# A delta-rule attention block on one core: x is fetched and added ahead of a batch's closing sums, and the gates of the next batch are spread over the second half of their step

## The chip, the cores and the metric

The kernel runs on one core of one Trainium2 chip. The metric is device time in microseconds (us) for one execution. Before the change the runs gave a median of 3071.77 us (three runs, 3068.05 to 3073.72).

## The reference, cut to what matters

The input x has 4 batches of 512 tokens of 512 features. The block is a chain of four parts, each of which reads the one before:

```
c   = bi_wkv(r=x, k=fside, v=fside, w, u, cond)        # scan over time, both ways
a   = gated_delta_rule(c)                              # W_qkvz, W_ba, conv of 4 taps, 16 q/k heads, 32 v heads
      g    = -exp(A_log) * softplus(a_proj + dt_bias)  # the gates, one per token and v head
      beta = sigmoid(b_proj)
      g summed within a chunk; T = (I + tril(beta k k' * exp(g_i - g_j)))^-1 ...
x1  = x + rmsnorm(o) * norm_w * silu(z) @ W_out'       # summed over all heads
h   = bi_wkv(r=x1, ...)                                # the second one, same form
out = x1 + h @ (sign(W) * mean|W|)' + bias             # a binarized weight
```

## The kernel before

**Units and steps.** The work of the attention is cut into units n = b*16 + hq: one batch and one q/k head, with its two v heads; there are 64. A unit is handled in chunks of 128 tokens, four to a batch. The kernel runs through steps i = 1 to 66, and step i works on several units at once: letters in the plan say how far off they are. F is unit i (projections, taps of the convolution, inverse), C is unit i-1 (the recurrence over four chunks), O is unit i-2 (norm and head turns), W is unit i-3 (the product with W_out), and K is unit i+6 (key norms and the matrix that is to be inverted). The units of a group of four are inverted together, in 30 small sub-steps on GpSimd, 1 to 20 in one step and 21 to 30 in the next; that comes every fourth step.

**The order is written by hand.** `plan` (L1173 to L1242) is a list of 22 slots, and in each slot a list of calls. All engines get their instructions in the order of these calls, through the helper `InOrder` (L75 to L80), so that each row of the profile says L80, and an operation is told by the names of its tiles. `job(i, slot, f, ...)` appends a further call behind those of a slot in step i. Items of the plan that begin with "wkv" or "gate" run only in the steps in which a slice of bi-WKV or the gates of the next batch are due; the gates come with head 8, which is in steps 8, 24 and 40, and prepare batches 1, 2 and 3.

**The gates.** `gates_product` (L305) puts the two projections of W_ba into PSUM (ps_ba). `gates_exp` (L321) makes beta's exponential, y and e = exp(-|y|). `gates_series` (L341) works out log(1+e) as a series on VectorE in three parts: 0 is s = e/(e+2) and its square, 1 is nine operations on p, and 2 is four operations that end in y, the gate. `gates_beta` (L336) finishes beta. `gates_sum` (L362) takes three matmuls that sum y within a chunk (ps_g). `gates_keep` (L369) makes eg = exp of those sums on ScalarE, a copy of the sums (gsum) on ScalarE, the negative copy (gsum) and a reordered copy (sp_f) on VectorE. `gates_turn` (L386) transposes sp_f on TensorE (ps_gt), and `gates_rows` (L391) copies it to rows and stores these in DRAM (gsc), from where each later unit loads its row, spread over all partitions, as dkd (`gap_load`, L593, through SyncE's queue). `gap_mask` (L601) masks dkd on GpSimd and `gap_exp` (L609) takes its exponentials on ScalarE, four instructions in each of two halves.

**The product with W_out and its closing sums.** It is done by a scheme of seven products of half size; `out_add` (L1034) adds the seven results of each unit into seven accumulators: parts 2 to 5 lie in xs[b], parts 1, 6 and 7 in sums[b]. When the last unit of a batch is through, `out_close` (L1055) turns these into the sum over heads: seven additions in the order of `CLOSE`, then four that add x, one for each row block of 128 tokens. `out_load` (L1051) fetches x for that into the tile x_again. xs[b] is then stored as x1[b] (for batches 0 to 2) through SyncE's queue, and the second bi-WKV and the last product work from it. The jobs at L1658 to L1663 place them: in step 18, 34 and 50 for batches 0, 1 and 2, and in step 65 for the last one, where the tail of the kernel follows (`last_turn`, `last_mix`, `last_product`, `last_add`).

**Buffers.** x_again uses the tag "raw" of pool `ld`, four buffers shared by the slices of bi-WKV (`load_slice`, L211) and a few weights. PSUM has banks "pj" (three), "pp" (two), "inv" (one) and "st" (two).

Other names that the prediction uses: `inverse_1` to `inverse_4` (L742 to L807) finish the inverse of unit F on TensorE with copies on VectorE (inv_t, nw); `key_norm` (L621) and `key_root` (L628) make 1/|k| from sums of squares, the start on VectorE (kn, rs_t_k, rs_y_k) and the iterations on GpSimd; `out_norm` and `out_root` (L972, L977) do so for the output (rs_y_o), and `out_scale` (L980) uses it; `taps` and `tap` (L515 to L529) are the convolution on VectorE (y); `z_product` (L857) the gate of the output (ps_z); `chunk_r`, `chunk_w` and `chunk_t` (L882 to L941) the recurrence, with tiles r, state, nw, qs and o.

Of the kernel before, what the change touches and what calls it, by code (L numbers as in the profile page):

```python
# [12 lines left out]
ALU = mybir.AluOpType  # L13
# [27 lines left out]
def kernel(  # L41
# [21 lines left out]
    B, S, D = x.shape  # L63
# [4 lines left out]
    NC = S // P  # L68
# [14 lines left out]
    V, A, G, T, Q = (InOrder(e) for e in (nc.vector, nc.scalar, nc.gpsimd, nc.tensor, nc.sync))  # L83
# [36 lines left out]
    for i in range(3):  # L120
        t = const.tile([P, NM, P], F32, name=f"inv_t{i}")
        G.memset(t, 0.0)
        inv_t.append(t)
        t = const.tile([P, NM // 2, 3 * BS], F32, name=f"inv_n{i}")
# [21 lines left out]
    with ExitStack() as main:  # L146
# [13 lines left out]
        xs, cT, beta, gsum, eg = {}, {}, {}, {}, {}  # L160
# [863 lines left out]
        def out_sum(b, i):  # L1024


            if i in (1, 6, 7):
                return sums[b][:, (1, 6, 7).index(i)]
            t, dh = {2: (0, 0), 3: (0, 1), 4: (1, 0), 5: (1, 1)}[i]
            return xs[b][:, 2 * t : 2 * t + 2, dh * D2 : (dh + 1) * D2]  # L1030

        sums = {}
# [13 lines left out]
            if i == 6:  # L1046
                del units[n]

        CLOSE = ((6, 1), (2, 1), (3, 5), (3, 6), (7, 6), (4, 7), (5, 7))

        def out_load(b, c):  # L1051
            raw = sums["x", c] = ld.tile([P, D], F32, tag="raw", name=f"x_again_{b}_{c}")
# [1 line left out]

        def out_close(b, i):  # L1055

            if i < len(CLOSE):
                to, more = (out_sum(b, j) for j in CLOSE[i])
                V.tensor_tensor(to, to, more, ALU.add)
                return  # L1060
            for c in (2 * (i - len(CLOSE)), 2 * (i - len(CLOSE)) + 1):
                V.tensor_tensor(xs[b][:, c], xs[b][:, c], sums["x", c], ALU.add)
            if i > len(CLOSE) and b < B - 1:
                Q.dma_start(out=x1[b], in_=xs[b])


# [97 lines left out]
        def last_add(b, c):  # L1164
# [7 lines left out]
        K, F, C, O, W = AHEAD, 0, -1, -2, -3  # L1172
# [14 lines left out]

            [(chunk_r, C, 1), (inverse_2, F), (out_add, W, 3), 
             (chunk_r_end, C, 1), (slab_end, K, 1), (chunk_q_end, C, 1),
             (gap_exp, F, "t", 1), ("gate", gates_series, 0), ("sub", 3, 23)],  # L1190

            [(out_product, W, 5), (project, K, 1, 0), (slab_turn, F, 2), ("wkv", turn_slice, "x"),
             (inverse_2_end, F), (out_add, W, 4), (out_scale, O, 1), ("wkv", wkv_bound), ("gate", gates_series, 1),
             ("sub", 4, 24)],

            [(chunk_w, C, 1), (project, K, 1, 1), (head_turn, O, 0), (out_product, W, 6), (chunk_w_end, C, 1), (out_add, W, 5), 
             (slab_end, F, 2), ("wkv", wkv_exp), ("wkv", wkv_x),
             (slab_start, F, 3), ("gate", gates_series, 2), ("gate", gates_beta), ("sub", 5, 25)],

            [(project, F, 2, 0), (out_add, W, 6), (tap, K, 1, 0), (taps, K, 1), (head_end, O, 0),  # L1200
             ("wkv", wkv_mix), ("sub", 6, 26)],

            [(chunk_t, C, 1), (inverse_3, F), ("gate", gates_sum), (chunk_t_end, C, 1), (silu, K, 1),
             ("wkv", wkv_scan, "d", False), (slab_start, F, 0), ("sub", 7, 27)],

            [(project, F, 2, 1), (head_turn, O, 1), (slab_turn, F, 3), ("gate", gates_keep), (inverse_3_end, F), ("wkv", wkv_scan, "d", True),
             (square, K, 1), (chunk_squares, C, 1), ("sub", 8, 28)],

            [(chunk_r, C, 2), (inverse_4, F), (norms, K, 1), (tap, F, 2, 0), (head_end, O, 1), (slab_end, F, 3), (tap, F, 2, 1),
             (chunk_r_end, C, 2), (tap, F, 2, 2), (tap, F, 2, 3), (norms_copy, K, 1), (chunk_q_end, C, 2),  # L1210
             ("wkv", wkv_sum, "d"), (slab_start, C, 4), (slab_start, C, 5), ("gate", gates_turn), ("sub", 9, 29)],

            [(project, F, 3, 0), (norms_turn, K, 1), (slab_turn, F, 0), (inverse_4_end, F), (silu, F, 2), ("gate", gates_rows),
             ("wkv", wkv_scan, "n", False), ("sub", 10, 30)],

            [(chunk_w, C, 2), (project, F, 3, 1), (chunk_w_end, C, 2), (key_norm, K), (key_root, K),
             (slab_end, F, 0), ("wkv", wkv_scan, "n", True), ("sub", 11, None)],

            [(project, F, 0, 0), (turn, F, 2), (tap, F, 3, 0), (taps, F, 3), ("store",), ("wkv", wkv_sum, "n"), (out_start, O, 0), ("sub", 12, None)],

            [(chunk_t, C, 2), (slab_turn, C, 4), (chunk_t_end, C, 2), (silu, F, 3),
             (turn_end, F, 2), ("soon", load_slice), ("wkv", wkv_under), ("sub", 13, None)],

            [(project, F, 0, 1), (turn, F, 1), (slab_turn, C, 5), (slab_end, C, 4),
             (chunk_squares, C, 2), (head_forms, O), (out_start, O, 1), ("sub", 14, None)],

            [(chunk_r, C, 3), (key_pairs, K), (tap, F, 0, 0), (slab_end, C, 5), (turn_end, F, 1),
             (tap, F, 0, 1), (chunk_r_end, C, 3), (tap, F, 0, 2), (tap, F, 0, 3),
             (chunk_q_end, C, 3), (inverse_load, F + 1), ("sub", 15, None)],

            [(z_product, C, 0, 0), (turn, F, 3), (key_matrix, K, 0), (silu, F, 0), ("sub", 16, None)],

            [(chunk_w, C, 3), (z_product, C, 0, 1), (out_turn, O, 0), (chunk_w_end, C, 3),
             (turn_end, F, 3), (square, F, 0), (key_matrix, K, 1), ("wkv", wkv_over, 0),
             (gap_load, K + 1, "d"), (slab_start, K + 1, 1), ("sub", 17, None)],

            [(z_product, C, 1, 0), (out_turn, O, 1), (out_end, O, 0), (key_blocks, K), ("wkv", wkv_over, 1), ("sub", 18, None)],

            [(chunk_t, C, 3), (norms, F, 0), (queries, F), (z_silu, C, 0), (out_end, O, 1),
             (out_forms, O), ("wkv", wkv_end), ("sub", 19, None)],  # L1240
# [15 lines left out]
        for pool, tag, count, shape in (  # L1256
# [3 lines left out]
            for i in range(count):  # L1260
                t = pool.tile(shape, F32, tag=tag, name=f"lent_{tag}_{i}")
# [6 lines left out]
        for pool, tag, shape in ((u1p, "nz", [P, NC, 2, HD]), (u1p, "hT", [P, 7, S // 2])):  # L1268
            t = pool.tile(shape, F32, tag=tag, name=f"lent_{tag}")
# [361 lines left out]
        def job(i, slot, f, *args):  # L1631
            jobs.setdefault((i, slot), []).append((f, args))
# [3 lines left out]
        for n in range(KT):  # L1636
            i, slot = at + n // 2, 9 * (n % 2)
# [3 lines left out]
        for b in range(B - 1):  # L1641
            i = at + 2 + 2 * b
# [15 lines left out]
        for b in range(B):  # L1658
            i = b * HQ + HQ + 2 if b < B - 1 else NU + 1
            for c in range(NC):  # L1660
                job(i, 6 + 3 * c, out_load, b, c)
            for n in range(len(CLOSE) + 2):
                job(i, 5 + n + max(0, n - len(CLOSE) + 1) * 3, out_close, b, n)  # L1663

        def last_step():
            n = NU - 1
# [40 lines left out]
        for i in range(1, NU - W - 1):  # L1707
            b, hq = divmod(i, HQ)
# [62 lines left out]
```

## Time and profile before

| | |
|---|---|
| runs before, median (lowest to highest) | 3071.77 us (3068.05 to 3073.72) |
| profiled execution, its own time | 3063.65 us |
| its span | 3061.9 us |
| mean granted TensorE clock | 0.982 |
| an ordinary step late in the run (step 56) | 42.34 us |
| steps with gates: 8, 24, 40 | 56.47, 53.43, 53.57 us |
| steps with a batch's sums: 18, 50 | 42.34, 42.34 us |
| the steps after these: 19, 35, 51 | 53.17, 53.17, 45.51 us |
| from the start of step 64 to the end | 79.9 us |

The profile is of one execution; it lies 8.1 us under the median of the runs. PE is the matmul engine (TensorE), PEld its weight loads, DVE is VectorE, ACT is ScalarE, POOL is GpSimd, SP is SyncE with its DMA queue. The first steps, with batch 0, last some 45.6 to 46 us each, as the products with the weights are accompanied by their preparation there. In a row of the timeline, "[3.14 <-ACT gsum L80]" means that the engine was idle for 3.14 us before that instruction, until ACT's instruction on gsum let it go. PEclk is the granted clock as a share of full speed.

### The profile page before, as it was taken

The page shows a single profiled execution, that of the slowest core. Times are in us where ns is not written, and L with a number is a line of the kernel's source. Part 1 is how long each engine was busy: PE and PEld are TensorE (multiplying, and loading weights), DVE is VectorE, ACT ScalarE, POOL GpSimd, SP SyncE. Part 2 cuts the span into 40 slices and gives each one's busy share as a digit, 9 for nine tenths or more (in the row PEclk, how much of TensorE's full clock was granted, in tenths as well). Part 3 has the DMA queues.
Part 4 walks back from the last instruction along what each step waited for, and adds up shares of the span by engine and source line. Part 5 has one row for each costly group of instructions (what it writes and reads, how often), then busy time and mean ns, then how long its engine had stood idle before and what let it go on. Part 6 is the DMA issues. An engine that isn't in the chain of part 4 may idle for free.

```text
span 3061.9 us, 60269 instructions
## 1 busy us (share of the span) xinstructions
PE 2949.3 (96%) x20816; PEld 2126.5 (69%) x20816; DVE 2279.0 (74%) x5101; ACT 1879.8 (61%) x5145; POOL 1479.1 (48%) x3249
## 2 busy tenths in 40 slices
PE   8689999999999999999999999999999999999998
PEld 4457776777777677677777677777777677766765
DVE  7858777778767788788867788788876767688754
ACT  3657666666666666666666566666666566656552
POOL 3126464564634556265543646356553525265313
PEclk9789999999999999999999999999999999999999
DMA  5325444454453433334333433434433332333422
GB/s 139 91 84 163 128 147 129 139 168 122 139 162 119 129 95 114 91 92 131 95 110 111 131 86 98 114 99 119 117 94 118 102 110 92 113 112 107 124 87 75
DMA packets 422464, 351.75 MB, mean 115 GB/s; under 512 B 219856, under 2 KB 337616, under 8 KB 421776
## 3 DMA queue, kind: packets, MB, share of 16 engines
q1 hardware_dynamic: 420240, 347.27, 38.6%
q8 instruction: 167, 2.74, 0.4%
q14 instruction: 137, 1.12, 0.1%
q10 hardware_dynamic: 1920, 0.62, 0.1%
HBM read 268.87 MB, written 78.91 MB: 114 GB/s over the span
## 4 chain that ended last, share of the span: by engine, by line
PE 77%; DVE 10%; ACT 5%; POOL 5%; issue 2%; DMA 2%; SPq 0%; POOLq 0%; ACTq 0%; DVEq 0%
PE ps_p L80 24%; PE ps_z L80 12%; PE ps_out L80 11%; PE ps_s L80 4%; PE ps_w L80 4%; PE ps_o L80 3%; DVE y L80 3%; PE ps_st L80 2%; PE ps_j L80 2%; PE ps_kq L80 2%; PE ps_f L80 2%; PE ps_kk L80 2%; PE ps_v L80 2%; PE ps_i L80 1%; POOL L L80 1%
## 5 line engine op out<-in xcount | busy, mean ns | idle before, releaser
L80 PE MATMUL ps_p<-cT,w 128*128 128x512 f32 x2000 | 955.1, 606 | 14.0 <-ACT w L80 11.7
L80 DVE SCALAR_TENSOR_TENSOR y<-ps_p,cw,y 128x511 f32<-128x511 f32 (+2 forms) x768 | 572.0, 745 | 268.7 <-ACT y L80 254.0
L80 PEld LDWEIGHTS ps_p<-cT,w 128*128 128x128 f32 x2000 | 358.1, 193 | 316.3 <-issue 271.3
L80 PE MATMUL ps_out<-wo,hS 128*128 128x256 f32 (+1 forms) x1780 | 462.2, 393 | 24.8 <-ACT k L80 14.0
L80 PE MATMUL ps_z<-w,cT 128*128 128x256 f32 x2048 | 478.0, 380 | 5.1 <-ACT w L80 5.1
L80 PEld LDWEIGHTS ps_z<-w,cT 128*128 128x128 f32 x2048 | 375.0, 191 | 48.3 <-ACT w L80 5.4
L80 PEld LDWEIGHTS ps_out<-wo,hS 128*128 128x128 f32 x1780 | 314.0, 192 | 74.1 <-ACT k L80 14.8
L80 ACT ACT_TABLE_LOAD x153 | 196.3, 1283 | 189.5 <-DVE y L80 167.7
L80 POOL TENSOR_TENSOR rs_t_k<-rs_y_k 128x4 f32<-128x4 f32 x171 | 56.8, 332 | 497.5 <-DVE rs_y_k L80 489.0
L80 POOL TENSOR_TENSOR L<-L,t 128x30 f32<-128x30 f32 (+14 forms) x450 | 250.8, 557 | 34.8
L80 DVE TENSOR_TENSOR x<-x,ps_out 128x512 f32<-128x512 f32 x240 | 163.2, 683 | 138.9 <-PE ps_out L80 138.8
L80 POOL TENSOR_TENSOR t<-L 128x30 f32<-128x30 f32 (+14 forms) x450 | 229.2, 509 | 30.9 <-DMA L<-blocks_m 0.4
L80 DVE SCALAR_TENSOR_TENSOR o<-o,rs_y_o,nz 128x128 f32<-128x128 f32 x512 | 196.8, 445 | 16.8 <-POOL rs_y_o L80 16.4
L80 ACT ACTIVATE qs<-ps_s,eg 128x128 f32<-128x128 f32 x384 | 119.9, 363 | 140.0 <-DVE r L80 114.3
L80 ACT ACTIVATE junk<-o 128x128 f32<-128x128 f32 x512 | 157.9, 308 | 75.2 <-DVE o L80 66.9
L80 ACT ACTIVATE y<-ps_p,cw 128x512 f32<-128x512 f32 x256 | 173.9, 680 | 48.0 <-PE ps_p L80 47.8
L80 ACT ACTIVATE dkt<-dkt,gsum 128x128 f32<-128x128 f32 x512 | 162.6, 392 | 58.1 <-POOL dkt L80 57.9
L80 ACT ACTIVATE v<-y 128x512 f32<-128x512 f32 x128 | 80.7, 630 | 189.5 <-DVE y L80 189.4
L80 ACT ACTIVATE wd<-ps_w,eg 128x128 f32<-128x128 f32 x384 | 118.5, 361 | 82.6 <-PE ps_w L80 82.2
L80 ACT ACTIVATE dkd<-dkd,gsum 128x128 f32<-128x128 f32 x512 | 156.4, 388 | 16.9 <-POOL dkd L80 16.2
L80 PEld LDWEIGHTS ps_o<-w,dkt 128*128 128x128 f32 x1024 | 154.2, 192 | 14.7 <-ACT w L80 2.1
L80 ACT COPY w<-ps_w 128x256 f32<-128x256 f32 (+1 forms) x346 | 144.7, 429 | 25.7 <-PE ps_w L80 25.6
(295 smaller groups left out, 5746.0 us busy)
## 6 DMA issues: line engine op xcount, KB each, us to landing
w<-wsc SPq DMA_DIRECT2D x288, 256.0 KB, 5.2
wo<-wosc SPq DMA_DIRECT2D x47, 896.0 KB, 5.0
dkd<-gsc SPq DMA_DIRECT2D x64, 512.0 KB, 4.1
dkt<-gsc SPq DMA_DIRECT2D x64, 512.0 KB, 5.0
wraw<-in_L_attn_W_qkvz_dram SPq DMA_DIRECT2D x96, 256.0 KB, 3.0
wsc<-w SPq DMA_DIRECT2D x90, 256.0 KB, 2.1
wosc<-wo SPq DMA_DIRECT2D x16, 896.0 KB, 3.9
blocks_m<-dkd SPq DMA_DIRECT2D x256, 32.0 KB, 1.9
```

The source lines that it names most:

```text
L80: return lambda *args, **kw: tc.keep_in_program_order(op(*args, **kw))
```

## The change

It moves calls between the slots; no operation is added or removed.

- The gates: series part 0 goes from slot 4 to slot 5, part 1 from slot 5 to slot 11, part 2 from slot 6 to slot 13; the sums from slot 8 to slot 14, right behind `chunk_t` of chunk 2; beta from slot 6 to 15; `gates_keep` from 9 to 16; `gates_turn` from 10 to 17, behind the first half of `z_product`; and the rows with their store from 11 to 19.
- The closing sums: x is fetched in slots 0 to 3, not 6, 9, 12 and 15. The sum (3, 5) comes first, then the four additions of x, then the other six sums: one call per slot, slots 7 to 17. Before, the seven sums stood in slots 5 to 11 and two pairs of additions of x in slots 15 and 19. The store of x1 moves with the last of them, from slot 19 to slot 17, which on SyncE's queue is ahead of dkd's load (slot 18), not behind it.

```diff
-             (gap_exp, F, "t", 1), ("gate", gates_series, 0), ("sub", 3, 23)],
+             (gap_exp, F, "t", 1), ("sub", 3, 23)],
...
-             (inverse_2_end, F), (out_add, W, 4), (out_scale, O, 1), ("wkv", wkv_bound), ("gate", gates_series, 1),
-             ("sub", 4, 24)],
+             (inverse_2_end, F), (out_add, W, 4), (out_scale, O, 1), ("wkv", wkv_bound), ("gate", gates_series, 0), ("sub", 4, 24)],
...
-             (slab_start, F, 3), ("gate", gates_series, 2), ("gate", gates_beta), ("sub", 5, 25)],
+             (slab_start, F, 3), ("sub", 5, 25)],
...
-            [(chunk_t, C, 1), (inverse_3, F), ("gate", gates_sum), (chunk_t_end, C, 1), (silu, K, 1),
+            [(chunk_t, C, 1), (inverse_3, F), (chunk_t_end, C, 1), (silu, K, 1),
...
-            [(project, F, 2, 1), (head_turn, O, 1), (slab_turn, F, 3), ("gate", gates_keep), (inverse_3_end, F), ("wkv", wkv_scan, "d", True),
+            [(project, F, 2, 1), (head_turn, O, 1), (slab_turn, F, 3), (inverse_3_end, F), ("wkv", wkv_scan, "d", True),
...
-             ("wkv", wkv_sum, "d"), (slab_start, C, 4), (slab_start, C, 5), ("gate", gates_turn), ("sub", 9, 29)],
-
-            [(project, F, 3, 0), (norms_turn, K, 1), (slab_turn, F, 0), (inverse_4_end, F), (silu, F, 2), ("gate", gates_rows),
-             ("wkv", wkv_scan, "n", False), ("sub", 10, 30)],
+             ("wkv", wkv_sum, "d"), (slab_start, C, 4), (slab_start, C, 5), ("sub", 9, 29)],
+
+            [(project, F, 3, 0), (norms_turn, K, 1), (slab_turn, F, 0), (inverse_4_end, F), (silu, F, 2),
+             ("wkv", wkv_scan, "n", False), ("gate", gates_series, 1), ("sub", 10, 30)],
...
+            [..., ("wkv", wkv_sum, "n"), (out_start, O, 0), ("gate", gates_series, 2), ("sub", 12, None)],
+            [(chunk_t, C, 2), ("gate", gates_sum), (slab_turn, C, 4), (chunk_t_end, C, 2), (silu, F, 3),
...
+             (chunk_squares, C, 2), (head_forms, O), (out_start, O, 1), ("gate", gates_beta), ("sub", 14, None)],
+             (chunk_q_end, C, 3), (inverse_load, F + 1), ("gate", gates_keep), ("sub", 15, None)],
+            [(z_product, C, 0, 0), ("gate", gates_turn), (turn, F, 3), (key_matrix, K, 0), (silu, F, 0), ("sub", 16, None)],
+            [..., (key_blocks, K), ("wkv", wkv_over, 1), ("gate", gates_rows), ("sub", 18, None)],
...
-        CLOSE = ((6, 1), (2, 1), (3, 5), (3, 6), (7, 6), (4, 7), (5, 7))
+        CLOSE = ((3, 5), (6, 1), (2, 1), (3, 6), (7, 6), (4, 7), (5, 7))
...
-            if i < len(CLOSE):
-                to, more = (out_sum(b, j) for j in CLOSE[i])
-                V.tensor_tensor(to, to, more, ALU.add)
+            if 1 <= i <= NC:
+                V.tensor_tensor(xs[b][:, i - 1], xs[b][:, i - 1], sums["x", i - 1], ALU.add)
                 return
-            for c in (2 * (i - len(CLOSE)), 2 * (i - len(CLOSE)) + 1):
-                V.tensor_tensor(xs[b][:, c], xs[b][:, c], sums["x", c], ALU.add)
-            if i > len(CLOSE) and b < B - 1:
+            to, more = (out_sum(b, j) for j in CLOSE[max(0, i - NC)])
+            V.tensor_tensor(to, to, more, ALU.add)
+            if i == NC + len(CLOSE) - 1 and b < B - 1:
                 Q.dma_start(out=x1[b], in_=xs[b])
...
             for c in range(NC):
-                job(i, 6 + 3 * c, out_load, b, c)
-            for n in range(len(CLOSE) + 2):
-                job(i, 5 + n + max(0, n - len(CLOSE) + 1) * 3, out_close, b, n)
+                job(i, c, out_load, b, c)
+            for n in range(NC + len(CLOSE)):
+                job(i, 7 + n, out_close, b, n)
```

## The prediction

> **What bounds the kernel now.** I read the page first, then stretches of the trace step by step. A step here runs from its first ps_w<-vb matmul to the next step's.
>
> ```profile
> span 3061.9 us, 60269 instructions
> ...
> PE 2949.3 (96%) x20816; PEld 2126.5 (69%) x20816; DVE 2279.0 (74%) x5101; ACT 1879.8 (61%) x5145; POOL 1479.1 (48%) x3249
> ```
>
> TensorE (PE) is busy 96% of the span, so only the steps in which PE idles can change. The busy times of step 56 (nothing special), 24 (gates), 19 and 51 (after a batch's sums), then three fixed clock windows (columns: stretch, length, PE, PEld, DVE, ACT, POOL, PEclk):
>
> ```profile
> 2622.08:2664.42 42.34, 42.34 (x310) 30.80 (x308) 27.46 (x71) 26.20 (x75) 10.61 (x35) 1.00 0.38 106
> 1221.17:1274.60 53.43, 48.60 (x348) 35.83 (x347) 35.53 (x96) 30.57 (x86) 10.96 (x35) 0.97 0.31 86
> 994.68:1047.85 53.17, 46.16 (x317) 33.35 (x316) 38.65 (x79) 29.37 (x77) 35.13 (x70) 0.90 0.38 117
> 2407.17:2452.68 45.51, 42.90 (x310) 30.79 (x309) 30.32 (x69) 27.70 (x76) 24.76 (x64) 1.00 0.42 122
> 1248.00:1251.41 3.41, 0.26 (x4) 0.14 (x5) 0.82 (x3) 3.35 (x9) 0.00 (x0) 1.00 0.00 0
> 1251.41:1254.83 3.42, 3.42 (x27) 1.90 (x27) 2.59 (x6) 2.12 (x7) 0.00 (x0) 0.50 0.02 5
> 2418.77:2422.19 3.42, 1.59 (x7) 1.11 (x8) 3.33 (x10) 2.23 (x10) 2.95 (x7) 1.00 0.00 0
> ```
>
> Step 56 is all PE: 42.34 us is the floor. The granted clock goes by windows of 3.41 us: PE busy 0.26 us in one, and the next is at half speed; busy 1.59, and it is not. A window with 1.30 (2760.11) was followed by 0.50 too. So a gap costs about 1.7 us more when it leaves a window under some 1.4 us of PE. Third, what PE waits for (total us, times, longest), and DVE in step 24:
>
> ```profile
> PE ps_out L80 <- ACT k L80: 14.0, 2, 7.0
> ...
> PE ps_j L80 <- issue: 6.3, 2, 3.2
> ...
> PE ps_w L80 <- DVE r L80: 3.7, 4, 2.6
> PE ps_lx L80 <- DVE x L80: 3.5, 1, 3.5
> ```
> ```profile
> 1250.38 0.29 DVE L80 TENSOR_SCALAR gsum<-ps_g 128x128 f32<-128x128 f32 x1 [3.14 <-ACT gsum L80]
> ```
>
> The 3.2s are steps 24 and 40: DVE holds at gates_keep's gsum until ACT has loaded a table and made eg and gsum; nw behind it is what PE wants. The 7.0s are steps 19 and 35, the 2.6 step 51, the 3.5 the tail.
>
> **Gates (steps 8, 24, 40).** Counts are unchanged; places change. Step 24 = 42.34 + ps_ba 3.64 + ps_g 0.74 + ps_gt 0.27 + idle 0.33, 1.34 and 3.15 (PE's rows) + 1.62 left for the half clock = 53.43.
>
> After: I lay the moved instructions over step 56, shifted by ps_ba's 3.64. DVE ends inverse_4's copies at +28.3 (2646.80 in step 56). Then, in program order, nine p operations 2.9 (starts 58.3 to 61.2 in the first gates), the key-norm trio 0.6, the taps of slab 3 2.3, and series part 2, 1.1: sp_y is ready at +35.1. PE reaches ps_g, now right behind chunk_t 2, at +32.4 (2650.82 in step 56). Idle 2.7. Later ps_gt stands behind the first half of z_0, reached at +41.4; it needs ACT's qs, a table load 1.28, eg 0.49, gsum 0.26, DVE's gsum and sp_f 0.57, ready at +43.0. Idle 1.6. The old 4.82 goes, 4.3 comes: 51.3 without a clock loss, -2.1 each in steps 24 and 40; step 8 (56.47, idle 4.04, same loss) -1.8. Sum -6.1. A 2.7 us gap leaves 0.7 us of a window if it lies inside one, 2.07 if split evenly: I take two drops of three, +3.4. Bounds: none, or three (+5.1). Net **-2.7** (-6.1 to -1.0; if ps_g and ps_gt found half my waits, -12.6). Cost nothing: ACT's table loads, four in the step in the order of instructions before and after; POOL's mask of steps 24 and 40, which that order puts ahead of key_root, since POOL is busy 11 us of 53 there; the rows' store, which goes out later on SP, behind the blocks' stores, but is first read by the dkd load of the next step, 40 us on (without that gap, its landing would hold the mask).
>
> **Batch sums.** Steps 18, 34, 50 have room on PE (42.34). The sums' price falls due one step on. The chain of waits of step 19, and POOL beside and without DVE's adds:
>
> ```profile
> 996.86 5.88 DMA w<-wsc
> 1002.73 0.07 issue
> 1002.80 1.10 POOL dkd L80
> ...
> 1006.37 0.48 ACT k L80
> 1006.84 0.04 issue
> 1006.89 3.78 PE ps_out L80 x8
> ```
> ```profile
> 989.53 1.28 DVE L80 TENSOR_TENSOR x<-x,x_again 128x512 f32<-128x512 f32 x2
> 989.70 1.63 POOL L80 TENSOR_TENSOR L<-L,t 128x238 f32<-128x238 f32 x1
> ```
> ```profile
> 994.98 0.66 POOL L80 TENSOR_TENSOR L<-L,t 128x238 f32<-128x238 f32 x1
> ```
>
> ACT's copy k, which PE waits for, is queued behind eight dkd exponentials; these wait for POOL's mask, queued behind the group's sub-steps and out_root. The dkd load is not it: issued 990.23, landed 994.23, mask 1002.80. POOL is late because sub-steps beside DVE adds of two SBUF tensors stretch: the four x adds (2.57 us) cost it 1.92, 0.75 us per us.
>
> After: x is loaded in slots 0 to 3, and all eleven adds come in slots 7 to 17. DVE is the same up to key_norm; then six adds instead of four stand beside POOL: 2 x 0.68 x 0.75 = +1.05. The mask also falls one root operation later, +0.28. PE idles 8.3 instead of 7.0: +1.3 in each of steps 19 and 35, with the clock's loss about equal (2.8 now, 2.6 then, +-0.85): **+2.6**. Between 0 (stretching ends in sub-steps that are waiting anyway) and +3.4 each. The x1 store, now ahead of the dkd load on SP's queue, holds it until the last add; 8.6 us of slack at the mask cover that; without them each us would be a us. r_3 in steps 18 and 34 waits for DVE at most 0.5: nothing taken.
>
> The Trainium skill ("SBUF — State Buffer", section "Who interferes with whom") says that DVE with two SBUF inputs and GpSimd share a port under an exclusive lock, and that the loser fully blocks. That speaks against the move; by one for one the 1.05 would be 1.36, the forecast 0.6 higher. The measured 0.75 lies under it.
>
> Step 51: PE waits 2.6 for r, behind DVE's out_scale, behind POOL's out_root. The same shift of some 0.8 makes it 3.4, and its window, 1.59 us busy now, falls to about 0.8: clock, +1.7. **+2.5** (0 to +2.7).
>
> **Tail.** x is issued at 3029.45 to 3031.4 and its adds end by 3037.21, PE idle 3.5, then a half clock (2.7 lost).
>
> ```profile
> 3034.25 0.69 DVE L80 TENSOR_TENSOR x<-x,x_again 128x512 f32<-128x512 f32 x1 [1.78 <-DMA x_again<-in_x_dram]
> ...
> 3037.21 1.87 DVE L80 TENSOR_TENSOR x<-x,ps_out 128x512 f32<-128x512 f32 x3
> ```
>
> After: x lies there, and DVE runs eleven adds at 0.68 without that wait, so the first x<-x,ps_out starts at about 3035.85: -1.35. The gap left, 2.2, is at the clock's edge: half of 2.7 saved. **-2.65** (-1.35 to -4.05).
>
> **Sum:** -2.7 + 2.6 + 2.5 - 2.65 = -0.25 on the profiled 3063.65, so 3063.4. The runs' median, 3071.77, lies 8.1 above that execution; the forecast on that scale is **3071.5**.
>
> **Rivals.** *Slower: POOL under DVE's adds.* The six adds cost POOL one for one (1.4, +0.28), and PE's longer gap empties a window more (+1.7): steps 19 and 35 +6.8, r_3 +0.5, step 51 +2.5, all three gate gaps drop the clock (-1.0), the tail gains 1.35 only: +7.4, **3079**. It decides once the gap in step 19 exceeds about 8.5. For it: gaps of 7.0 already halved three windows. Against: the 0.75, and sub-steps with slack.
>
> *Faster: the gates fit.* What decides is DVE's backlog at +28; its row in step 56, 1.31 idle before slab 3's taps, can absorb part of the p operations. Waits halve to 2.15 a step, no drops: -12.6; step 51 unchanged and clock kept in the tail: +2.6 - 4.05. -14, **3058**. If nothing of what is said to be spread waits at all: 6 more off, 3051.
>
> *Clock by gap length.* Only gaps over a whole window drop it: the gates keep 3.4, step 51 1.7, the tail's 2.2 gap keeps 1.35 more. -6.7, **3065**. Against it: the window with 1.30 us of PE, and step 24's gap of 3.15, which dropped it. The Trainium skill ("TensorE: Matmul & The Clock Gate", "HAM oscillation — how this bites in real kernels") gives this rule: "no PE-idle gaps >~3.4µs." By it the time is this rival's; the 3.15 gap does not agree.
>
> *The change does not do what it says:* x's adds simply trade places with sums, DVE's total is the same; that is in the forecast already (closes +5.1, no gain).
>
> **How the numbers follow.** Forecast 0.50, 3066 to 3077; slower 0.24; gates fit 0.14; gap length 0.12. A measurement tells about 0.2%, 6.1 us, from no change. Faster: 0.14, half of 0.12, and 0.03 of the forecast's edge: 0.23. Slower: 0.24 and 0.02 of the forecast's edge: 0.26. Same: 0.51. For 8 in 10 the range leaves out the gates-fit case and the upper end of POOL's: 3063 to 3080.
>
> **What would show it.** Step 24 near 51.3 to 53, with PE waits at ps_g (2.7, DVE sp_y) and ps_gt (1.6, DVE sp_f) and none at ps_j; steps 19 and 35 near 54.5 with 8.3 at ps_out; step 51 near 48; PE reaching ps_lx some 1.3 earlier. A step 19 of 43, or gate steps of 47, would make me wrong towards faster: then the mask, or the p operations, weren't what I think PE waits for. Steps 18, 34 or 50 over 44 would make me wrong towards slower.

## The result and the profile after

The changed kernel takes 3053.48 us (median of 4 runs, 3052.29 to 3055.59), the kernel before 3072.74 in the runs beside it (4 runs): ratio 0.994, 95% interval 0.9923 to 0.9958. It is faster by about 0.6%, the interval leaves out no change, and the time lies 9.5 us under the low end of the range. The first four runs of the kernel before were on the high side: in later sets of 21 and 22 runs its median was 3066.35 and 3066.63, and in a further set the changed kernel came to 3052.60 beside 3067.49 (ratio 0.9959, 0.9946 to 0.9973). So the gain is some 14 to 15 us, or 19 by the first runs. The two profiled executions, 3063.65 and 3053.92, differ by 9.7 us.

Second profiles of both kernels were taken (3068.99 and 3052.60). Lengths of the steps by which they differ, in us:

| steps | before (two profiles) | changed (two profiles) | forecast of the change | measured, mean |
|---|---|---|---|---|
| 19 and 35 | 106.4, 106.8 | 96.9, 96.8 | +2.6 | -9.7 |
| 18, 34 and 50 | 127.0, 127.0 | 129.2, 129.2 | 0 | +2.2 |
| 51 | 45.5, 44.9 | 44.4, 44.4 | +2.5 | -0.8 |
| 8, 24 and 40 | 163.5, 165.7 | 161.0, 161.1 | -2.7 | -3.5 |
| 9 | 46.8, 46.7 | 47.6, 47.7 | 0 | +0.9 |
| 64 to the end | 79.9, 79.4 | 77.8, 76.2 | -2.65 | -2.7 |

The rest is the start and single half-clock windows in steps 1 to 7 and 58 to 62, which come and go between executions of one kernel. In total the gates and the tail came out much as forecast. The closing part is where the forecast failed.

The page of the changed kernel, and then steps 24, 19 and 51 of it, with the columns as in the prediction:

```profile
span 3052.2 us, 60274 instructions
...
PE 2945.0 (96%) x20816; PEld 2124.5 (70%) x20816; DVE 2285.3 (75%) x5101; ACT 1881.6 (62%) x5145; POOL 1475.2 (48%) x3249
```
```profile
1214.16:1267.69 53.53, 48.89 (x349) 35.74 (x348) 36.48 (x96) 30.93 (x86) 11.38 (x35) 0.97 0.31 88
992.41:1040.84 48.43, 44.97 (x317) 32.16 (x316) 39.69 (x79) 29.28 (x77) 34.61 (x69) 0.96 0.43 130
...
2397.19:2441.61 44.42, 43.06 (x309) 30.84 (x308) 31.28 (x71) 27.47 (x76) 24.36 (x63) 1.00 0.47 141
```

The count of instructions on each engine is the same; step 24 is as long as before, and step 19 has lost 4.7 us, with a granted clock of 0.96 in place of 0.90. What PE waits for in the changed kernel, from the list of waits (total us, times, longest):

```profile
PE ps_out L80 <- DVE sums L80: 10.3, 4, 3.5
...
PE ps_g L80 <- DVE sp_y L80: 8.0, 3, 3.3
...
PE ps_gt L80 <- DVE sp_f L80: 4.1, 3, 1.4
...
PE ps_lx L80 <- DVE x L80: 2.1, 1, 2.1
```

The two waits of 7.0 us for ACT's k are gone from the list; in their place PE waits 3.5 for DVE's copy of sums. In step 19 of the changed kernel, first PE, then ACT:

```profile
997.45 1.89 PE L80 MATMUL ps_out<-wo,hS 128*128 128x256 f32 x8
...
1004.35 1.26 PE L80 MATMUL ps_out<-wo,hS 128*128 128x256 f32 x4 [3.46 <-DVE sums L80]
```
```profile
1001.26 2.44 ACT L80 ACTIVATE dkd<-dkd,gsum 128x128 f32<-128x128 f32 x8 [4.77 <-POOL dkd L80]
1003.61 0.56 ACT L80 COPY k<-ps_k 128x512 f32<-128x512 f32 x1
```

ACT still waits for POOL's mask and still copies k last, at 1003.61. But PE does not wait for that: the fourth and fifth product (ps_out x8) run at 997.45, right behind ps_k. Before, the same eight matmuls stood until 1006.89:

```profile
1006.89 3.78 PE L80 MATMUL ps_out<-wo,hS 128*128 128x256 f32 x8 [7.00 <-ACT k L80]
```

The mask starts 50.8 us after the start of step 18 (50.5 before), so the gain is not an earlier mask.

What differs is in the compiled program. The tiles ps_out, ps_k, ps_x and others share three banks of PSUM, and which bank a tile gets is settled when the program is laid out. In steps 19 and 35, in order:

| | product 0 | 1 | 2 | ps_k | product 3 | 4 | 5 |
|---|---|---|---|---|---|---|---|
| before, bank | 0 | 2 | 0 | 1 | **1** | 2 | 0 |
| changed, bank, step 19 | 1 | 0 | 1 | 2 | **0** | 1 | 0 |

Before, product 3 was put into the bank of ps_k, and so could not start until ACT, ps_k's reader, had copied it, behind eight exponentials that waited for POOL's mask. In the compiled program of the kernel before, the first matmul of product 3 does wait for ACT's copy k; after the change it waits for an earlier instruction of DVE. Of all 28 steps of the kernel before that have a ps_k, only 19 and 35 have it so. After the change the late mask is off PE's path, and the next thing late is POOL's out_root, which DVE's out_scale waits for, with the copy of sums behind it.

### The profile page after: what moved, and what is told of

Its sections match the earlier page's. It is cut to its first block, busy times and chain, and to the rows that moved or that the text cites. A ratio compares the mean times of both kernels' runs of the same rounds, so it can differ in the third digit from the quotient of the medians.

```text
span 3052.2 us, 60274 instructions
## 1 busy us (share of the span) xinstructions
PE 2945.0 (96%) x20816; PEld 2124.5 (70%) x20816; DVE 2285.3 (75%) x5101; ACT 1881.6 (62%) x5145; POOL 1475.2 (48%) x3249
## 4 chain that ended last, share of the span: by engine, by line
PE 75%; DVE 10%; POOL 5%; ACT 5%; DMA 2%; issue 2%; SPq 0%; POOLq 0%; ACTq 0%; DVEq 0%
PE ps_p L80 23%; PE ps_z L80 12%; PE ps_out L80 11%; PE ps_w L80 4%; PE ps_s L80 4%; DVE y L80 3%; PE ps_o L80 3%; PE ps_st L80 2%; PE ps_j L80 2%; PE ps_kq L80 2%; PE ps_f L80 2%; POOL t L80 2%; POOL L L80 2%; PE ps_v L80 1%; PE ps_i L80 1%
## 5 line engine op out<-in xcount | busy, mean ns | idle before, releaser
L80 PE MATMUL ps_p<-cT,w 128*128 128x512 f32 x2000 | 958.2, 608 | 16.0 <-ACT w L80 13.6
L80 POOL TENSOR_TENSOR rs_t_o<-rs_y_o 128x8 f32<-128x8 f32 x192 | 38.6, 201 | 256.9 <-DVE rs_y_o L80 232.8
```

Source lines behind the costliest of these rows:

```text
L80: return lambda *args, **kw: tc.keep_in_program_order(op(*args, **kw))
```

## The experiments

Theory A was: the bank is what counts, and the earlier store of x1 is what moves it. Rival B: it is the additions' order, by POOL. Rival C: the gates bring more than their steps show.

**The two parts alone.** Close: only the functions `out_close` and `CLOSE` and the jobs are from the changed kernel. Gates: only the plan.

```diff
-                job(i, 6 + 3 * c, out_load, b, c)
+                job(i, c, out_load, b, c)
...
+                job(i, 7 + n, out_close, b, n)
```
```diff
-            [(chunk_t, C, 1), (inverse_3, F), ("gate", gates_sum), (chunk_t_end, C, 1), (silu, K, 1),
+            [(chunk_t, C, 1), (inverse_3, F), (chunk_t_end, C, 1), (silu, K, 1),
...
+            [(chunk_t, C, 2), ("gate", gates_sum), (slab_turn, C, 4), (chunk_t_end, C, 2), (silu, F, 3),
```

> The kernel before with the closing sums alone moved (new order, x fetched in slots 0 to 3, all eleven additions in slots 7 to 17, store of x1 in slot 17); the gates stay. Theory A: the gain of the closing part comes from which PSUM bank the fourth product of steps 19 and 35 gets: before, that of ps_k, whose reader on ACT is queued behind the masked exponentials; with the store of x1 earlier, another. It expects steps 19 and 35 near 48.4 (53.2 before), steps 18, 34 and 50 some 0.7 longer, step 51 about 1 shorter, the tail 2 shorter: about 10 to 16 us faster than before. Rival B: the additions' new order keeps POOL from being late; the same times, but the mask some 2 us earlier against the start of step 18. Rival C: the gates carry the gain: under 5 us here.

> The kernel before with the gates alone spread; closing sums, x and store as before. Theory A: steps 24 and 40 stay near 53.5 (idle at ps_g about 3.3 and at ps_gt about 1.4 in place of 0.33, 1.34 and 3.15), step 8 falls by 2 to 3; steps 19 and 35 stay near 53.2 as ps_k and the fourth product share a bank there: 1 to 5 us faster in all. Rival C: 9 us or more faster, being the part of the gain that the one profile of before does not show.

Close alone: 3058.06 us against 3066.63, ratio 0.9975 (0.9963 to 0.9986); steps 19 and 35 are 48.3 and 48.2, steps 18, 34 and 50 together 129.2, step 51 44.5. 8.6 us faster, a little under the 10 expected. Gates alone: 3062.38, ratio 0.9988 (0.9979 to 0.9997), 4.3 us faster; step 8 falls from 56.5 to 53.7, steps 24 and 40 stay at 53.7, and steps 19 and 35 stay at 52.8 and 52.6 with the wait for k (7.2). The parts add up: 8.6 + 4.3 = 12.9 of 14. Rival C falls.

**The second pair of additions, and with it the store of x1, earlier in the kernel before.**

```diff
-                job(i, 5 + n + max(0, n - len(CLOSE) + 1) * 3, out_close, b, n)
+                job(i, 5 + n + max(0, n - len(CLOSE) + 1) * 3 - 2 * (n == len(CLOSE) + 1), out_close, b, n)
```

> The kernel before with one thing moved: the second pair of additions of x and with it the store of x1 from slot 19 to slot 17; the seven sums, the gates and the fetches of x stay. Theory A: the fourth product of steps 19 and 35 gets another bank than ps_k, so PE's 7.0 us wait for ACT's k goes and a wait of some 3.5 us for DVE's copy of sums comes; steps 19 and 35 near 48.5 to 50, 6 to 10 us faster in all. Rival B (the additions' order and POOL's lateness): the additions still stand behind the sums, so steps 19 and 35 stay near 53 and the time within 2 us of before.

3060.88 against 3066.63, ratio 0.9983 (0.9974 to 0.9991): 5.8 us, just under the 6 expected. Steps 19 and 35 fall to 48.6 and 48.8, product 3 is in another bank than ps_k, and PE waits in step 19 for

```profile
1008.49 2.08 PE L80 MATMUL ps_out<-wo,hS 128*128 128x256 f32 x4 [3.84 <-DVE sums L80]
```

as in the changed kernel. POOL's mask starts 8.1 us after the start of step 19, as late as in the kernel before, and the additions of x still stand behind the sums: rival B does not explain this gain. One job two slots up gives nearly all of the change's gain in these two steps, 9.2 us; steps 8, 24 and 40, which the edit does not touch, are together 2.3 longer in this profile than in the two of before.

**The store put back, in the changed kernel.**

```diff
-            if i == NC + len(CLOSE) - 1 and b < B - 1:
-                Q.dma_start(out=x1[b], in_=xs[b])
+            job(i, 19, out_store, b)
```

> The changed kernel with one thing put back: the store of x1 in slot 19, behind the load of dkd. Theory A: the fourth product of steps 19 and 35 shares ps_k's bank again; PE waits 7 us or more for ACT's k, steps 19 and 35 back near 53, about 9 us slower than the changed kernel. Rival B: the additions keep their new order, so steps 19 and 35 stay near 48.4 and the time within 2 us of the changed kernel.

3052.37 (3066.63 before beside it; ratio 0.9954, 0.9941 to 0.9966), and steps 19 and 35 are 47.2 each. This was a miss: product 3 is indeed in ps_k's bank again (bank 2 both in step 19), yet nothing of the 9 us comes back. Theory A alone is not enough. PE's row in step 19, and POOL's mask:

```profile
1000.20 1.99 PE L80 MATMUL ps_out<-wo,hS 128*128 128x256 f32 x8 [0.67 <-ACT k L80]
```
```profile
990.93 1.09 POOL L80 TENSOR_SCALAR_AFFINE_SELECT dkd<-dkd 128x1024 f32<-128x1024 f32 x1
```

PE waits for k, as the bank has it, but 0.67 us and not 7. The dkd load is issued 15.9 us ahead of step 19's start here (4.5 in the kernel before), and the mask stands between the sub-steps of step 18, 3.4 us ahead of step 19's start, not behind out_root. That the load is early because x's buffers come free early is likely, but not shown. Rival B's times came true in this run, and in part for its reason, as POOL is not late with the mask; but in the changed kernel itself the mask is as late as before. So theory D: it takes both, the shared bank and the late mask.

**k copied ahead of the exponentials.** If D is right, the wait must also go with the bank shared and the mask late, when ACT's copy of k no longer stands behind the exponentials. First in all steps that have a slice of bi-WKV:

```diff
-             (out_norm, O), (out_root, O), (gap_mask, K, "d"), ("load",)],
+             (out_norm, O), (out_root, O), (gap_mask, K, "d"), ("wkv", turn_slice, "k"), ("wkv", wkv_copy), ("load",)],
```

> The kernel before with ps_k turned at the end of slot 0 and its copy k on ACT put ahead of the masked exponentials of dkd; sums, x, store and gates as before. The fourth product of steps 19 and 35 still gets ps_k's bank, and POOL's mask is as late as before. Theory D (it takes both, a mask that is late and a bank shared with ps_k, since only then does PE wait behind ACT's exponentials): the 7.0 us wait for k goes, the chain by out_root and out_scale is left with some 3.5; steps 19 and 35 near 48 to 49.5, 6 to 10 us faster than before. Rival (PE would wait for the mask's exponentials anyway, by another tile): steps 19 and 35 stay over 52.

Steps 19 and 35 come to 49.6 and 47.9, as D has it. But the time is a miss, 3076.54 against 3067.49, ratio 1.0033 (1.002 to 1.0045), 9 us slower: nearly every other step with a slice becomes 0.5 us or more longer (steps 20 and 21 43.7, not 43.2). The same in steps 19 and 35 alone:

```diff
+                    elif f in ("two", "not"):
+                        if w and (f == "two") == (i in (19, 35)):
+                            rest[0](w, *rest[1:])
```

> The kernel before with ps_k turned and copied ahead of dkd's exponentials in steps 19 and 35 alone. The mask stays late, the fourth product stays in ps_k's bank. Theory D: steps 19 and 35 at 47.5 to 49.7 (53.2 before), all other steps as before, 7 to 11 us faster than before. Rival (DVE's or POOL's work holds these steps anyway): they stay over 52.

3059.36 against 3066.35, ratio 0.9981 (0.9972 to 0.9991): 7.0 us faster, steps 19 and 35 at 49.6 and 49.3. In the compiled program ps_k and product 3 still share a bank. In step 19 the mask is still late, but the twelve matmuls of products 3 to 5 run ahead of it, first POOL, then PE:

```profile
1005.40 1.09 POOL L80 TENSOR_SCALAR_AFFINE_SELECT dkd<-dkd 128x1024 f32<-128x1024 f32 x1
```
```profile
1001.87 2.86 PE L80 MATMUL ps_out<-wo,hS 128*128 128x256 f32 x12
```

The rival of this run falls. D holds in these cases: shared and late 7.0 us of wait, other bank and late 3.5 (another chain), shared and early 0.7, shared and late but k copied first none for k.

**Both kernels again.**

> The kernel before, unchanged, timed against itself: within 0.15% of 1. Its second profile shows how far two executions of one kernel differ by where half-clock windows fall: if the first profile (3063.65) fell on few of them, this one shows one to four more (1.7 us each) in steps 51, 60 and 62, where PE's gaps are at the clock's edge, and the steps sum to 3064 to 3072.

> The changed kernel once more, for a second profile of it and for its time beside the others on one chip: steps 19 and 35 within 0.3 of 48.4, steps 24 and 40 within 1.7 (one clock window) of 53.6; 10 to 20 us faster than before.

Before: 3066.55 against 3066.35, ratio 1.0003 (0.9994 to 1.0012); single runs from 3061 to 3075. Its second profile is at half clock for 52.4 us from step 3 to the last instruction, the first for 42.4, as expected more, though in steps 8, 40 and 58 and not in 51, 60 and 62. Changed: 3052.60 against 3067.49; 27.3 and 21.9 us at half clock in its two profiles. One profile of this kernel is good to some 5 us, and differences under that are read from steps, not from the total.

**What is left.** The changed kernel still idles 3.5 us in steps 19 and 35 behind POOL, and 4.6 in the gate steps. If x is added a step earlier, DVE is less in POOL's way:

```diff
+            early = 1 if b < B - 1 else 0
-                job(i, c, out_load, b, c)
+                job(i - early, c, out_load, b, c)
+                if early and 1 <= n <= NC:
+                    job(i - 1, 6 + n, out_close, b, n)
```

> The changed kernel with x fetched and added a step earlier (steps 17, 33 and 49, slots 0 to 3 and 7 to 10), so that only seven sums are left in steps 18, 34 and 50 (slots 7 to 13), and the store of x1 in slot 19, behind dkd's load; the last batch is as in the changed kernel. If DVE's additions are what holds up r and stretches POOL's sub-steps, steps 18, 34 and 50 fall back to 42.3, out_root ends 1.5 to 2 us earlier, and steps 19 and 35 come to 44.5 to 46.5: 5 to 9 us faster than the changed kernel. If POOL is late for another reason, steps 19 and 35 stay at 47 to 48.5.

This kernel adds x to part 5 before the sum (3, 5) reads it, so its part 3 takes up x of part 5 as well, and what it computes is not the block; its instructions are the same in number. Steps 18, 34 and 50 are back at 42.4, 42.4 and 42.6, steps 19 and 35 at 46.4, step 51 at 43.2, as expected. It is also theory D's last case: in step 19 product 3 is in another bank than ps_k, the mask starts 11.2 us ahead of the step, and PE does not wait for k. But the time is 3053.30 (3047.86 to 3055.61) beside 3052.60 for the changed kernel, a miss: the steps' 7 us do not show in the median of five runs (the profile is of the fastest, 3047.86), and why stays open.

> The last one, with the gates' sums in slot 16 in place of 14, gates_keep in slot 18, gates_turn in slot 20 and the rows' store in slot 21. If what PE waits for at ps_g is the series on DVE, ready at about +35.7, and at ps_gt the keep on ACT, both are covered by PE's own work now: steps 24 and 40 near 47 to 48.5, step 8 near 51, 12 to 17 us faster than with x moved alone. If DVE has no room and the wait only moves to a later tile, under 6 us.

The same computation as the last one, gates moved on:

```diff
-            [(chunk_t, C, 2), ("gate", gates_sum), (slab_turn, C, 4), (chunk_t_end, C, 2), (silu, F, 3),
+            [(chunk_t, C, 2), (slab_turn, C, 4), (chunk_t_end, C, 2), (silu, F, 3),
...
+             (chunk_q_end, C, 3), (inverse_load, F + 1), ("gate", gates_sum), ("sub", 15, None)],
```

3038.66 beside 3067.49 (ratio 0.9908, 0.9894 to 0.9921), 15 us under it. Steps 24 and 40 are 48.7 and 48.9, a little over the 48.5 expected, step 8 50.5; PE's only wait in step 24 is 1.7 for state, behind series part 2 on DVE. Step 9 takes 3.7 back (51.0, not 47.3): PE waits 2.6 there for ACT's w, behind the exponentials of dkt (the tile like dkd that belongs to unit F), whose load is issued 2.9 us into the step, not 1.1, and lands 6.1 us after that. Then with x split so that the sum (3, 5) reads what it should, and part 2 one slot on:

```diff
+                at = slice(0, D2) if b < B - 1 and c > 1 else slice(0, D)
...
+                V.tensor_tensor(xs[b][:, c, D2:], xs[b][:, c, D2:], sums["x", c][:, D2:], ALU.add)
...
+             (turn_end, F, 2), ("soon", load_slice), ("wkv", wkv_under), ("gate", gates_series, 2), ("sub", 13, None)],
```

> The changed kernel with x fetched a step earlier and added there, but for the part that the sum (3, 5) still has to read, which is added right behind that sum; the store of x1 in slot 19; the gates' sums in slot 16, series part 2 in slot 14, keep in 18, turn in 20, rows in 21. Steps 19 and 35 at 46 to 47, steps 18, 34 and 50 at 42.3 to 42.6, step 51 near 43.2, steps 24 and 40 at 47 to 48 (PE's wait for state falls from 1.7 by the 1.1 that part 2 takes): 12 to 18 us faster than the changed kernel.

3038.92 (3038.37 to 3040.28) against 3066.35: ratio 0.9917 (0.9904 to 0.9931), 27 us under the kernel before and 14 under the changed one. The steps are as expected, but for 18 and 50 at 42.8 and 42.7. PE's wait in step 24 fell to

```profile
PE ps_s L80 <- DVE state L80: 0.6, 1, 0.6
```

from 1.7, by the 1.1 of part 2, and the step is 47.6. At last these places of the gates alone, in the plan of the changed kernel:

> The changed kernel with the gates alone moved on: series part 2 in slot 14, sums in slot 16, keep in 18, turn in 20, rows in 21; the closing sums, x and the store of x1 as in the changed kernel. If the waits at ps_g and ps_gt are what the gate steps still cost, steps 24 and 40 come to 47.5 to 48.2, step 8 to 50.5 with step 9 some 3 longer: 9 to 14 us faster than the changed kernel, so that most of the 14 us between it and the version with x split is the gates'. If the earlier x carries that version, under 6 us.

3043.39 (3037.52 to 3045.32) against 3065.69, ratio 0.9921 (0.9908 to 0.9935): 9 us under the changed kernel; steps 24 and 40 47.6 each, step 8 50.5, step 9 52.4 (4.7 longer, not 3). So the gates carry 9 of the 14. Steps 18, 19, 34, 35, 50 and 51 are together 7.6 longer here than with x split, in one profile of each; of that the medians show 4.5, which four and five runs do not settle.

## Why the prediction was wrong, step by step

**The step that failed:** "PE idles 8.3 instead of 7.0: +1.3 in each of steps 19 and 35". I took it as given that PE waits for ACT's k, and worked out only how late the mask would be. That PE waits for k at all hung on product 3 lying in ps_k's bank, and the earlier store of x1 took that away. The row said so: a matmul that reads wo and hS waited for ACT's k, which it does not read. Here the wait was for the place it writes to, as the banks show. The chain of waits went on from there to the mask, and I followed it without asking why its first link was there. Measured in step 19: idle 3.46 and not 8.3. Of the 4.74 us that the step lost, 3.54 are idle (7.00 - 3.46), and for the other 1.2 PE was less long busy, with 3.4 us of the step at half clock in place of 10.2. By the steps, the change made -13.6 us where the sum has -0.25; 12.3 of the difference are in steps 19 and 35. Why the layout chose that bank is argued, not shown: product 1's copy into x waits for x1's store to end, as DVE's row of step 19 before tells,

```profile
998.65 0.69 DVE L80 COPY x<-ps_out 128x512 f32<-128x512 f32 x1 [1.70 <-DMA x<-x]
```

so with a late store ps_k's bank may have looked free sooner. Against it stands the version with x a step earlier: its store is in slot 19 too, the same copy waits 0.92 for it, and yet product 3 of step 19 is not in ps_k's bank. So the slot of the store alone does not settle the bank.

**POOL's stretch** was mis-sized: I took +1.05 for two more additions (1.02 by its own factors). From the start of key_root to the last sub-step POOL took 20.86 us before and 20.93 after. So six additions one by one cost about as much as four in pairs. In the changed kernel, two additions and the sub-step beside each:

```profile
986.15 0.68 DVE L80 TENSOR_TENSOR x<-x,sums 128x512 f32<-128x512 f32 x1
```
```profile
986.34 0.97 POOL L80 TENSOR_TENSOR t<-L 128x238 f32<-128x238 f32 x1
```
```profile
982.40 0.67 POOL L80 TENSOR_TENSOR L<-L,t 128x220 f32<-128x220 f32 x1
```
```profile
982.52 1.10 DVE L80 TENSOR_TENSOR sums<-sums 128x512 f32<-128x512 f32 x1
```

The first sub-step took 0.97 in place of 0.61, 0.36 more; the pair of 1.28 us shown in the prediction cost 1.63 - 0.65 = 0.98. What POOL lost is what was left of DVE's work when the sub-step started, less 0.13: 986.83 - 986.34 = 0.49 for the single addition, 990.81 - 989.70 = 1.11 for the pair. In the second case the sub-step started first and kept its time, and the addition took 1.10 in place of 0.68. So a price per us of DVE (0.75) does not carry over from pairs to single additions: it goes by which of the two starts first. The full block that the Trainium skill gives ("SBUF — State Buffer", "Who interferes with whom"), for the one that issues second, is within 0.13 us of these rows. One for one, 0.68 for a single addition, would be too much.

**Steps 18, 34 and 50**, costed at nothing: 0.73 each, +2.2. In step 18 PE falls back 0.57 at the product that waits for r_3, just beyond the 0.5 bound, and 0.16 at ps_kq, which waits for DVE's dkd and which I had not counted. **Step 51**, forecast +2.5: -0.8. I had not counted that the changed order puts the dkd mask (1.09) behind out_root, where before it stood ahead of it, inside key_root of step 50; r's wait fell from 2.6 (2.0 in the second profile) to 1.4, and no clock window was lost.

**Gates:** right in mechanism, and the total is near (-3.5, forecast -2.7), in part by luck. ps_g waited 3.3 in steps 24 and 40 (2.7 forecast) and 1.4 in step 8, ps_gt 1.4 (1.6), nothing at ps_j, with one clock drop each in steps 24 and 40 and none in step 8. Steps 24 and 40 changed by +0.1 and -0.6, where the forecast, -2.1 and a clock drop of 1.7, makes -0.4 each; step 8 gained 3.0, not 1.8. (The sum's own terms for step 8, idle from 4.04 to 4.3 and a loss of 1.62, make -1.4, not -1.8.) DVE's row in step 24:

```profile
1242.69 3.34 DVE L80 SCALAR_TENSOR_TENSOR sp_p<-sp_p,sp_e 128x128 f32<-128x128 f32 x8
```

The eight p operations took 3.34 us here, 0.42 apart, where I had taken the spacing of the first gates. **Tail:** ps_lx waited 2.1 (2.2 forecast), and time at half clock from step 64 on fell from 8.3 and 8.0 us to 3.4 and 1.5. The step's -2.7 against -2.65 is the mean of -2.1 and -3.3.

**The scale:** adding 8.1 us to go from the profile to the median was of no weight for the difference, but three runs gave a median 5 us above that of 21, and these 5 are part of the 18 us between 3071.5 and 3053.48.

**The rival of gap length** falls by all traces: see the last section.

## What to carry to other kernels

When an engine waits for a tile that its instruction does not read, look first at the place it writes: find out whether the two share a buffer or bank before working out how late the other is, and ask of each moved transfer whether it moves the choice of buffers. Here a small change of order (5.8 us) or a copy taken out of a queue in two steps (7.0) was enough, with the late mask as late as before. Where a wait is to be covered, put the waiting instruction behind what the engine can do meanwhile, here two slots on, and look what is next on the engine that was late.

## What the runs showed of the hardware

The granted clock goes by fixed windows of 3.41 us. In 14 profiles, of windows at full clock, from step 3 on, all in which PE was busy under 0.44 of the window (1.5 us) were followed by one at half clock, and none in which it was over 0.52 (1.77 us); between these, some were. A gap of 2.5 us was enough when it lay inside one window (step 9 of the version with x split: window busy 0.26), and 2.61 was not when it was shared between two (step 51 before). So the same gap costs 1.7 us or nothing by where it falls, and executions of one kernel differ in part for that: the two profiles of the kernel before have 42.4 and 52.4 us at half clock from step 3 on, and the second takes 3.3 longer there. The rule of the Trainium skill ("TensorE: Matmul & The Clock Gate", "HAM oscillation — how this bites in real kernels"), "no PE-idle gaps >~3.4µs", is too wide for these runs: gaps of 2.1 and 2.5 us inside one window were followed by half clock.
